# Four state-space mixers: steps of their own for the strung-out side work of the first chunk

## The chip, the cores and the metric

The kernel is one program on one core of a Trainium2 chip. The metric is the device time of the whole program in microseconds (us); for the kernel before it is 7736.49, the median of three runs (7729.43 to 7759.1).

## What is computed

The input is a batch of 64 images of 11 x 11 places and 128 channels. Four layers follow each other; each adds a mixer and then a feed-forward part to its input. The mixer is the same in all four layers, a selective state-space model that runs over 256 places (the inner channels) in two directions k, with 121 channels d (the image's places) and 16 states n:

```python
xz = x @ in_proj_w.T                         # x layer-normalised
xc, z = jnp.split(xz, 2, axis=-1)
xc = silu(conv1d(xc, conv_w) + conv_b)       # 3 taps
x_dbl = einsum('bkdl,kcd->bkcl', stack([t, t]), x_proj_w)
delta = softplus(einsum('bkrl,kdr->bkdl', dts, dt_proj_w) + dt_proj_b)
dA, dBu = exp(delta * A), delta * Bs * xs
_, h = associative_scan(_ssm_combine, (dA, dBu), axis=3)
y = einsum('bkdln,bknl->bkdl', h, Cs) + Ds * xs
y = y[:, 0] + flip(y[:, 1], axis=-1)
out = layernorm(y) * gelu(z) @ out_proj_w.T
```

The feed-forward parts (a mixture of experts, two recurrent networks, a spectral filter) are not touched by the change.

## The kernel before, in words

**Chunks, directions, steps.** A mixer (class `Conv`, method `run`) works on 8 images at a time, so there are 8 chunks. A chunk has two directions; the main loop counts them through as m = 2 x chunk + direction. In a direction the 121 channels are taken two at a time: 61 pairs, and each pair is one step of the main loop. So a chunk has 122 steps (`STEPS`) and a mixer 976. All 128 partitions hold 16 states x 8 images.

**What one step does.** TensorE (PE) spreads `delta` of a channel from the tile `R` to the 128 partitions, into one of five PSUM buffers `da` (`rows`, L686). ScalarE (ACT) takes its exponential with A as scale (`exps`, L699). This is done three steps ahead. VectorE (DVE) scans two channels at once (`scan`, L707) with `da` and `ub`, into a column of `H` or `HX`. A tile `ub` of four channels, so of two steps, is loaded by a broadcast DMA from `uD` in DRAM (`load_u`, 512 KB, ten steps ahead, six buffers), and GpSimd (POOL) multiplies it by B (`times_b`, L675, five steps ahead). A buffer of `ub` comes free when the scan of the step before the load is done, so SyncE (SP), which issues all these DMAs in program order, waits there for DVE at every second step. After every 16 steps PE multiplies the finished columns by C (`by_c`, L728) bit by bit, and ACT (first direction) or DVE (second) takes the sum out of PSUM (`keep_y`).

**What must be ready for a direction.** `dD` in DRAM holds delta as three bfloat16 parts that add up to it, `uD` holds delta x input, `bcD` holds B and C. `R`, `ub`, `Bt` and `Cp` are loaded from them (`load_r`, `load_u`, `load_bc`). The method `steps(c, k, at)` makes `dD` and `uD` for chunk c and direction k, in four parts of two images: projection on PE (`project`), a copy out of PSUM (`keep`), one softplus for all four on ACT (`soft`: a load of the activation table, the function, a load of the table for exponentials), then for each pair of images: `first`, `second` and `third` on ACT make the three parts of `d` (L329, L346, L358), `rest` and `less` on PE subtract in between, `u` on POOL (L333), and `store` issues the two DMAs to `dD` and `uD`. The tiles `d` and `u` have two buffers each, so pair 2 takes that of pair 0 and pair 3 that of pair 1.

**Side work and its places.** While chunk c is scanned, the next chunk is prepared between the scans: its input `x` is loaded (`begin`), normalised over channels (`stats` and `scales` on DVE, `scales2` and `normal` on ACT), transposed (`turn`, `turned`), convolved on PE and copied to the tile `t` (`conv`, `convd`), put through SiLU (`silu`), and then comes `steps` for both directions. The method `aside` makes B and C of the next chunk (`bc`: PE, ACT, a store) and its skip term (`skip`: a scaling on ACT into PSUM, L406, and then a combination on DVE, L409).

Each piece gets a step. `at` puts it into the plan, `lay_at` does so for a list with steps given, `lay` spreads a list evenly over a stretch and rounds down to whole steps. Within a step the main loop emits the reading-out of PSUM, the rows and first exponential of the step three ahead, the loads and B products that are due, the scan, then the plan's pieces in the order of their (fractional) steps, then the second exponential. As every engine and SP works in the order in which it is given work, a step is a place in several queues at once.

For chunks 1 to 7 the steps come from the table `AT`, with one start and one distance for each kind of piece. Chunk 0 is special: a mixer begins by making its own first direction ahead of the main loop, and the second direction (`self.steps(0, 1, ...)`) and the skip term are done within the steps of chunk 0, beside the next chunk's preparation. The steps for this stretch stand as numbers in `run`. In the list that `steps` takes, the numbers are: first projection, distance between projections, softplus, first of the splitting, distance between the pairs; relative to the pair's start, `first` comes 1, `rest` 3, `u` 4, `second` 5, `third` 7 and `store` 12.5 steps later. The normalisation's pieces come relative to their start: statistics from -3, `scales` 3, `scales2` 6, `scales3` 8, `normal` from 10, the transposes and their copies 13.5 to 19.5.

Of the kernel before, what the change touches and what calls it, by code (L numbers as in the profile page):

```python
# [70 lines left out]
def act_tables(nc, which):  # L71
# [8 lines left out]
CB = 8  # L80
# [4 lines left out]
RING = 5  # L85
UB = 6
AT = {
    "x": -12.5, "st": -3, "mv": 3, "sc2": 6, "sc3": 8, "nm": 10, "tn": 13.5, "td": 15.5, "tn2": 17.5,
    "td2": 19.5, "cv": 20, "cve": 49, "silu": 52, "p0": 53, "pa0": 3.75, "s0": 66, "b0": 66, "ba0": 7.875,
    "p1": 100, "pa1": 2.25, "s1": 109, "b1": 111, "ba1": 7.5, "u": 4, "d0": 1, "r": 3, "d1": 5, "l": 6.5,  # L90
    "d2": 7, "dst": 12.5, "bc": 54, "bca": 3, "sk": 99, "ska": 2.5, "y0": 15.5, "y1": 35, "y2": 57.5, "y3": 82,
    "k0": 27, "k1": 44.5, "k2": 66.5, "k3": 89, "ka": 2, "ks": 2.5, "km": 4.5, "k2s": 6.5, "k3s": 9, "kn": 11,
    "kg": 13, "xa": 28.5, "xb": 66, "g0": 38, "z0": 77, "g1": 81.5, "z1": 109, "ga": 5, "za": 3.5, "gt": 117.5,
    "gta": 2, "ge": 126.5, "cz": 8, "cza": 3.75, "lbc": -18, "lu": 10, "tb": 5, "ys": 8, "ysa": 1, "ysh": 8,
    "r0": -10, "r1": 2, "r2": 23, "r3": 37,
}


class Conv:
# [679 lines left out]
    def run(self):  # L779
        NC, G = self.NC, 2 * self.NC * PAIRS  # L780
        self.R, self.bc, self.ub, self.pre = {}, {}, {}, {}
        NT = 2 * NC * TILES
        first = [PAIRS * (T // TILES) + 2 * (T % TILES) for T in range(NT)]

        begin, norms, convs = self.lead(0)
        aside = self.aside(0)
        self.do([begin] + [f for _, f in norms] + convs)
        bc = [(3 * i // 3 + 1.5, f) for i, f in enumerate(aside[: 3 * CB // 2])]
        self.do([f for _, f in sorted(self.steps(0, 0) + bc, key=lambda x: x[0])])
        for x in self.da:  # L790
            self.nc.vector.memset(x[:, :, 0:1], 0.0)
        self.lay(aside[3 * CB // 2 :], 0, 20)
        self.lay_at(self.steps(0, 1, (0, 2, 9, 11, 6)))
        for c in range(NC):
            s = STEPS * c
            if c + 1 < NC:
                begin, norms, convs = self.lead(c + 1)
                aside = self.aside(c + 1)
                bc, skip = aside[: 3 * CB // 2], aside[3 * CB // 2 :]
                if c == 0:  # L800
                    self.at(2, begin)
                    self.lay_at([(18 + i, f) for i, f in norms])
                    self.lay([f for _, f in convs[:-1]], 40, 64)
                    self.at(65, convs[-1][1])
                    self.lay_at(self.steps(1, 0, (67, 2, 76, 77, 6)))
                    self.lay_at(self.steps(1, 1, (106, 2, 115, 116, 6)))
                    self.lay(bc, 78, 90)
                    self.lay(skip, 93, 104)
                else:
                    self.at(s + AT["x"], begin)  # L810
                    self.lay_at([(s + i, f) for i, f in norms + convs])
                    for k in range(2):
                        at = [s + AT[f"p{k}"], AT[f"pa{k}"], s + AT[f"s{k}"], s + AT[f"b{k}"], AT[f"ba{k}"]]
                        self.lay_at(self.steps(c + 1, k, at))
                    self.lay_at([(s + AT["bc"] + AT["bca"] * (i // 3) + i % 3, f) for i, f in enumerate(bc)])
                    self.lay_at([(s + AT["sk"] + AT["ska"] * (i // 3) + i % 3, f) for i, f in enumerate(skip)])
            self.lay_at([(s + i, f) for i, f in self.gate(c)])
            if c > 0:
                self.lay_at([(s + i, f) for i, f in self.tail(c - 1)])
        for m in range(2 * NC):  # L820
            s = PAIRS * m
            self.at(max(s + AT["lbc"], 0), lambda m=m: self.load_bc(m))
            for u in range(4):
                self.at(s + AT["cz"] + AT["cza"] * u, lambda m=m, u=u: self.own_c(m, u))
            for dq, (p0, n) in enumerate(DQ):

                before = s + AT[f"r{dq}"]
                self.at(max(before, 0), lambda m=m, dq=dq: self.load_r(m, dq))

                after = s + p0 + n  # L830
                nxt = DQ[(dq + 1) % 4][1]
                for h in range(4):
                    step, n_steps = after + h * nxt // 4, (nxt - 1) // 4 - 1 + (nxt == 16)
                    for i in range(8):
                        self.at(step + i * n_steps // 8, lambda m=m, dq=dq, slot=8 * h + i: self.by_c(m, dq, slot))
                    keep = lambda m=m, dq=dq, h=h: self.keep_y(m, dq, h)
                    step += n_steps
                    self.pre.setdefault(step, []).append(keep)
            if m % 2:
                for half in range(2):  # L840
                    for q in range(4):
                        for j in range(2):
                            self.at(
                                s + PAIRS + AT["ys"] + AT["ysh"] * half + AT["ysa"] * q,
                                lambda m=m, h=half, q=q, j=j: self.store_y(m, h, q, j),
                            )
        sides, load, ahead, finish = self.last(NC - 1)
        self.at(G + 1, sides)
        self.at(G + 12, lambda: load(0))

        early = {}
        for T in range(NT):
            for lead, f in ((AT["lu"], self.load_u), (AT["tb"], self.times_b)):
                step = first[T] - lead
                early.setdefault(max(step, -1), []).append(lambda T=T, f=f: f(T))
        self.do([f for _, f in self.plan.pop(0)])
        self.do(early.pop(-1))
        for g in range(3):
            self.rows(g)
            self.exps(g, 0)  # L860
            self.exps(g, 1)
        for g in range(G + 60):
            self.do(self.pre.pop(g, []))
            if g < G:
                if g + 3 < G:
                    self.rows(g + 3)
                    self.exps(g + 3, 0)
                self.do(early.pop(g, []))
                self.scan(g)
            self.do([f for _, f in sorted(self.plan.pop(g, []), key=lambda x: x[0])])  # L870
            if g + 3 < G:
                self.exps(g + 3, 1)
        assert not self.plan and not early and not self.pre
        ahead()
        load(1)
        X = self.cx.X
        for c in range(NC - 1):
            self.nc.sync.dma_start(X[:, CB * c : CB * c + CB, :], self.dst(CB * c, CB))
        finish()
        self.nc.sync.dma_start(X[:, CB * NC - CB :, :], self.dst(CB * NC - CB, CB))  # L880
# [614 lines left out]
```

## Time and profile before

| What | us |
|---|---|
| median of the three runs | 7736.49 |
| the profiled execution's own time | 7752.68 |
| its span, first to last instruction | 7750.9 |
| of this, before the first mixer's first scan | 69.5 |
| mixer 1, first to last scan | 1475.3 |
| feed-forward part 1 and the next mixer's beginning | 349.1 |
| mixer 2 | 1469.9 |
| feed-forward part 2 and beginning | 295.5 |
| mixer 3 | 1474.5 |
| feed-forward part 3 and beginning | 303.0 |
| mixer 4 | 1481.6 |
| feed-forward part 4 | 832.5 |

The rows between the first and the last are times between scans in the trace. PE is busy 78% of the span, DVE 73%, ACT 70% and POOL 68%; over the mixers alone (second mixer) PE is busy 1151.8 us, DVE 1294.1, ACT 1234.6 and POOL 1304.6 of 1469.9, and the 16 DMA engines 93%. Chunk by chunk, from one chunk's first scan to the next one's (the last to its last scan's end), the second mixer takes 197.7, 185.6, 183.5, 183.2, 182.7, 183.3, 180.9 and 173.0 us.

How to read this: the page counts an engine as busy while it executes, and names for its idle time what ended it. In a kernel in which all engines hand work round in a ring, the share of busy time says little; what counts is, step by step, which engine or transfer the scan waited for.

### The profile page before, as it was taken

Reading aid. Unit: us, or ns where it says so; the run is one execution under the profiler, and the core shown is the slowest. Engines: PE = TensorE matmul, PEld = TensorE weight load, DVE = VectorE, ACT = ScalarE, POOL = GpSimd, SP = SyncE. Lnnn points to the kernel's source line nnn. Section 1 sums busy time; section 2 is a strip of 40 time slices with the busy share of each in tenths; the row PEclk is TensorE's granted clock in tenths of the full one; section 3 lists DMA queues with packets and bytes.
Section 4 is the critical chain, followed back from the end, with each engine's and each line's share of the span. In section 5 each row is a group of like instructions: output and inputs, shape, how many; then the busy total and the mean of one; then the engine's idle time right before and its main releaser. Section 6 shows DMA issues by size and latency. Waiting matters only on the chain. (4 is left out here: it accounts for less than half of the span.)

```text
span 7750.9 us, 208787 instructions
## 1 busy us (share of the span) xinstructions
PE 6041.0 (78%) x84334; PEld 3448.5 (44%) x84334; DVE 5659.8 (73%) x7849; ACT 5449.4 (70%) x12343; POOL 5293.3 (68%) x2659
## 2 busy tenths in 40 slices
PE   6788778776788877766788888767678887758999
PEld 3444444465344444444344444434344444434445
DVE  5888888844788888962788888871788888872201
ACT  7888888733888888853788888862788888852200
POOL 6798999812888888931888888940888898960000
PEclk8888898777898989875889989875788888879999
DMA  7899999856899999942899999951899999971111
GB/s 181 227 247 243 245 246 243 215 167 170 221 241 249 246 240 244 247 110 75 220 241 244 246 248 243 243 140 37 217 236 243 243 245 241 245 184 46 35 39 36
DMA packets 905471, 1536.54 MB, mean 198 GB/s; under 512 B 136840, under 2 KB 617442, under 8 KB 904503
## 3 DMA queue, kind: packets, MB, share of 16 engines
q1 hardware_dynamic: 903223, 1521.09, 76.3%
q8 instruction: 662, 10.85, 0.6%
q14 instruction: 306, 2.51, 0.1%
q10 hardware_dynamic: 1280, 2.10, 0.1%
HBM read 1265.98 MB, written 256.97 MB: 196 GB/s over the span
## 5 line engine op out<-in xcount | busy, mean ns | idle before, releaser
L675 POOL TENSOR_TENSOR ub<-ub,Bt 128x1024 f32<-128x1024 f32 (+1 forms) x1984 | 4557.2, 2323 | 589.7 <-DMA ub<-uD 447.1
L699 ACT ACTIVATE da<-da,A 128x255 f32<-128x255 f32 x7744 | 3291.7, 451 | 696.1 <-PE da L686 612.0
L707 DVE TENSOR_TENSOR_SCAN H<-da,ub 128x512 f32<-128x512 f32 x2048 | 2391.8, 1208 | 354.4 <-POOL ub L675 183.9
L707 DVE TENSOR_TENSOR_SCAN HX<-da,ub 128x512 f32<-128x512 f32 (+1 forms) x1856 | 2130.4, 1190 | 318.5 <-POOL ub L675 160.1
L686 PE MATMUL da<-R,pick 120*128 120x255 bf16 x7744 | 1658.9, 305 | 546.0 <-DVE H L707 277.3
L686 PEld LDWEIGHTS <-pick 120*128 120x128 bf16 x7744 | 662.9, 103 | 1494.6 <-issue 1054.9
L728 PE MATMUL yb<-H,Cz 128*16 128x64 f32 x32768 | 782.2, 236 | 187.7 <-ACT yst L745 107.7
L728 PE MATMUL yb<-HX,Cz 128*16 128x64 f32 x32768 | 813.4, 237 | 122.6 <-DVE HX L707 62.7
L728 PEld LDWEIGHTS yb<-HX,Cz 128*16 128x16 f32 x32768 | 531.3, 105 | 641.9 <-issue 338.1
L728 PEld LDWEIGHTS yb<-H,Cz 128*16 128x16 f32 x32768 | 540.9, 103 | 584.0 <-issue 313.3
L263 PE MATMUL pc<-w_conv,xnT 128*121 128x256 f32 x1344 | 458.7, 433 | 27.4 <-ACT d L358 18.6
L184 POOL MEMSET t<- 128x2048 f32 x4 | 7.2, 1805 | 599.6 <-PE px L1221 211.8
L313 PE MATMUL pd<-t,w_dt 122*128 122x512 f32 x480 | 317.6, 749 | 101.7 <-ACT t L274 55.1
L745 ACT COPY yst<-yb 128x512 f32<-128x512 f32 (+2 forms) x640 | 334.9, 551 | 83.9 <-DMA yD<-yst 70.2
L743 DVE TENSOR_TENSOR yst<-yst,yb 128x512 f32<-128x512 f32 (+2 forms) x640 | 337.1, 543 | 73.7 <-PE yb L728 73.2
L340 PE MATMUL pr<-sp,ident 128*128 128x512 f32 x480 | 302.7, 717 | 80.0 <-ACT sp L301 75.0
L333 POOL TENSOR_TENSOR u<-sp,t 128x512 f32<-128x512 f32 x240 | 307.6, 1282 | 33.9 <-DMA uD<-u 32.8
L1294 DVE COPY U<-pu 128x488 f32<-128x488 f32 x128 | 85.4, 667 | 282.5 <-PE pu L1327 282.5
L1296 ACT COPY U<-pu 128x488 f32<-128x488 f32 x128 | 72.9, 570 | 308.7 <-PE pu L1327 308.7
L652 POOL TENSOR_TENSOR Cz<-Cp,own 128x512 f32<-128x512 f32 x256 | 275.5, 1076 | 0.0
L329 ACT CAST d<-sp 128x512 bf16<-128x512 f32 x240 | 148.6, 619 | 172.1 <-DMA dD<-d 171.9
L263 PEld LDWEIGHTS pc<-w_conv,xnT 128*121 128x121 f32 x1344 | 211.7, 194 | 94.9 <-ACT d L358 25.0
(237 smaller groups left out, 7243.8 us busy)
## 6 DMA issues: line engine op xcount, KB each, us to landing
ub<-uD SPq DMA_DIRECT2D x1920, 512.0 KB
dD<-d SPq DMA_DIRECT2D x256, 384.0 KB
R<-dD SPq DMA_DIRECT2D x192, 420.0 KB
uD<-u SPq DMA_DIRECT2D x256, 256.0 KB
yD<-yst SPq DMA_DIRECT2D x512, 60.5 KB
y<-yD SPq DMA_DIRECT2D x112, 242.0 KB
bcD<-bc SPq DMA_DIRECT2D x128, 128.0 KB
w1g<-in_L_ffn_weight_dram SPq DMA_DIRECT2D x16, 1024.0 KB
```

Of the source, the lines that this page charges most:

```text
L263: nc.tensor.matmul(pc, lhs, rhs, start=(j == 0), stop=(j == taps - 1))
L313: nc.tensor.matmul(s["p"], self.w_dt[:, k, :], tb[: D + 1], start=True, stop=True)
L333: nc.gpsimd.tensor_mul(s["u"], s["sp"], tb)
L340: nc.tensor.matmul(s["pr"], self.cx.ident, s["sp"], start=True, stop=False, skip_group_check=True)
L652: self.nc.gpsimd.tensor_mul(self.Cz[u], C.unsqueeze(2).to_broadcast([128, 64, CB]), self.own.unsqueeze(1).to_broadcast([128, 64, CB]),)
L675: self.nc.gpsimd.tensor_mul(x, x, self.bc[m, "Bt"].unsqueeze(1).to_broadcast([128, n, L]))
L686: self.nc.tensor.matmul(self.da[g % RING][:, j, 1:], self.pick[:n, d % 5].rearrange("p n b -> p (n b)"), self.R[m, d // 35][:n, d % 35 // ...
L699: self.nc.scalar.activation(x, x, AF.Exp, scale=self.A[:, m % 2, d : d + 1])
L707: self.nc.vector.tensor_tensor_scan(self.H[dq % 2][:, :n, p - DQ[dq][0]], self.da[g % RING].rearrange("p j l -> p (j l)")[:, :n], x.rearra ...
L728: self.nc.tensor.matmul(self.yb[32 * q : 32 * q + 16, slot % 8, :, :, :w], self.Cz[slot // 8][:, place % 64 : place % 64 + 2, :].rearrange ...
L743: nc.vector.tensor_add(dst, dst, src)
L745: nc.scalar.copy(dst, src)
```

## The change

The change lets the pieces of chunk 0 (its own second direction and skip term, and the preparation of chunk 1) take their steps from a table `AT0`, with a start and a distance for each kind, as `AT` has them for later chunks. The work itself, its engines and its buffers stay. `AT` is written in other lines with the same numbers; `strung` is a small function that lays three pieces a step apart and the next three by a distance of its own, as the code for later chunks did before.

```diff
+AT0 = {
+    "x": 1, "n": 10.5, "cv": 39.5, "cve": 63.5, "silu": 64, "p": 0, "pa": 2, "s": 10, "b": 10, "ba": 7, "p0": 67.5,
+    "pa0": 2.75, "s0": 78, "b0": 78, "ba0": 6.25, "p1": 104.5, "pa1": 1.875, "s1": 112.5, "b1": 113.5, "ba1": 6.625,
+    "bc": 79, "bca": 3.375, "sk": 94, "ska": 3.25, "k": 0, "ka": 3,
+}
...
-        self.lay(aside[3 * CB // 2 :], 0, 20)
-        self.lay_at(self.steps(0, 1, (0, 2, 9, 11, 6)))
+        F = AT0
+
+        def strung(fs, at, apart):
+            self.lay_at([(at + apart * (i // 3) + i % 3, f) for i, f in enumerate(fs)])
+
+        strung(aside[3 * CB // 2 :], F["k"], F["ka"])
+        self.lay_at(self.steps(0, 1, [F[x] for x in ("p", "pa", "s", "b", "ba")]))
...
-                    self.at(2, begin)
-                    self.lay_at([(18 + i, f) for i, f in norms])
-                    self.lay([f for _, f in convs[:-1]], 40, 64)
-                    self.at(65, convs[-1][1])
-                    self.lay_at(self.steps(1, 0, (67, 2, 76, 77, 6)))
-                    self.lay_at(self.steps(1, 1, (106, 2, 115, 116, 6)))
-                    self.lay(bc, 78, 90)
-                    self.lay(skip, 93, 104)
+                    self.at(F["x"], begin)
+                    self.lay_at([(F["n"] + i, f) for i, f in norms])
+                    apart = (F["cve"] - F["cv"]) / (len(convs) - 1)
+                    self.lay_at([(F["cv"] + i * apart, f) for i, (_, f) in enumerate(convs[:-1])])
+                    self.at(F["silu"], convs[-1][1])
+                    for k in range(2):
+                        self.lay_at(self.steps(1, k, [F[x + str(k)] for x in ("p", "pa", "s", "b", "ba")]))
+                    strung(bc, F["bc"], F["bca"])
+                    strung(skip, F["sk"], F["ska"])
```

Step by step, in chunk 0:

| Piece | before | after |
|---|---|---|
| own skip (DVE half) | 1, 6, 11, 16 | 1, 4, 7, 10 |
| own softplus | 9 | 10 |
| own splitting, start and distance | 11, 6 | 10, 7 |
| chunk 1: load of x | 2 | 1 |
| chunk 1: normalisation's start | 18 | 10.5 |
| chunk 1: convolutions | 40 to 63 | 39.5 to 62.8 |
| chunk 1: SiLU | 65 | 64 |
| chunk 1, first direction: projections | 67, then every 2 | 67.5, then every 2.75 |
| softplus; splitting | 76; 77, every 6 | 78; 78, every 6.25 |
| second direction: projections | 106, then every 2 | 104.5, then every 1.875 |
| softplus; splitting | 115; 116, every 6 | 112.5; 113.5, every 6.625 |
| chunk 1: B and C, stores at | 80, 83, 86, 89 | 81, 84.375, 87.75, 91.125 |
| chunk 1: skip (DVE half) | 93, 96, 99, 102 | 95, 98.25, 101.5, 104.75 |

## The prediction

> **What bounds the kernel now.** I read the table of slices first, then the scans (L707) one by one, then the waits and the timeline where their pace breaks. Each mixer runs 976 scans, 122 per chunk of 8 images; I call the stretch from one scan's start to the next a step and count from the mixer's first scan.
>
> ```profile
> DVE  5888888844788888962788888871788888872201
> ACT  7888888733888888853788888862788888852200
> POOL 6798999812888888931888888940888898960000
> DMA  7899999856899999942899999951899999971111
> ```
>
> The four plateaus are the mixers. Inside one, chunk 0 takes longest: 196.2, 197.7, 196.9 and 197.7 us from its first scan to chunk 1's, where chunk 4 takes 183.0, 182.7, 183.5 and 183.6. So the place of this change is four stretches of 197 us, 10% of the run. Stage by stage, in the second mixer (columns: the window and its length; busy us of PE, weight loads, DVE, ACT, POOL with counts; granted clock, DMA share, GB/s):
>
> ```profile
> 1893.90:1926.00 32.10, 19.33 (x114) 8.86 (x114) 26.84 (x33) 25.52 (x53) 28.86 (x15) 0.61 0.97 225
> 1926.00:1952.40 26.40, 18.54 (x301) 9.35 (x299) 18.89 (x26) 18.75 (x47) 25.35 (x14) 0.77 0.82 218
> 1952.40:1992.40 40.00, 37.23 (x640) 22.06 (x639) 35.16 (x32) 33.18 (x77) 34.21 (x16) 0.96 0.97 252
> 1992.40:2021.30 28.90, 19.21 (x298) 8.29 (x299) 16.93 (x15) 25.23 (x51) 26.41 (x15) 0.82 0.64 165
> 2038.50:2066.10 27.60, 16.52 (x251) 8.21 (x251) 20.45 (x22) 17.94 (x42) 19.93 (x10) 0.72 0.79 208
> 2066.10:2091.70 25.60, 20.09 (x342) 9.48 (x341) 21.94 (x29) 19.82 (x41) 16.69 (x9) 0.90 0.96 233
> 2091.70:2277.20 185.50, 148.16 (x2533) 83.98 (x2535) 163.79 (x208) 161.24 (x365) 165.97 (x84) 0.90 0.94 242
> ```
>
> The rows are steps 0 to 20, 20 to 35, 35 to 66, 66 to 80, 92 to 106, 106 to 122, and all of chunk 1. The last row shows the limit of a good stretch: DMA at 0.94. In chunk 0 DMA is free in steps 20 to 35, 66 to 80 and 92 to 106 (0.82, 0.64, 0.79) and full around them. Time can be won only where DMA is free: by my sum of its packets 6.4 us of idle lie in steps 15 to 35, 13.1 in 65 to 85, 6.1 in 90 to 105. What stands there are in-order queues. The second mixer's chunk 0, ACT's and DVE's waits:
>
> ```profile
> ACT da L699 <- PE da L686: 21.6, 22, 2.2
> ACT d L329 <- DMA dD<-d: 15.6, 3, 5.6
> ...
> DVE H L707 <- ACT da L699: 7.3, 5, 4.2
> DVE skip L409 <- ACT ps L406: 6.7, 3, 4.8
> DVE HX L707 <- POOL u L333: 4.4, 1, 4.4
> ...
> DVE r L202 <- ACT r L198: 4.0, 1, 4.0
> ```
>
> Two kinds are to be seen. ACT has to copy image pair 2 into the buffer of pair 0 (two buffers of d) and waits three times, 5.6 us at most, for pair 0's store. And DVE has strung work (skip, r) ahead of its scans that waits for ACT:
>
> ```profile
> 1909.50 1.91 ACT L301 ACTIVATE sp<-sp 128x2048 f32<-128x2048 f32 x1
> 1911.43 1.28 ACT L73 ACT_TABLE_LOAD   x1
> ...
> 1914.17 0.75 DVE L409 SCALAR_TENSOR_TENSOR skip<-t,Ds,ps 121x512 f32<-121x512 f32 x1 [4.77 <-ACT ps L406]
> ```
>
> The softplus with its two table loads (1.28 + 1.91 + 1.28 us) holds ACT for 4.5 us; the skip behind it holds the scans.
>
> **Part by part.** No instruction is added or removed; the sums are of waits. Rows are the second mixer's.
>
> (a) *Own skip and the next chunk's statistics, ahead of the softplus.* Skips go from steps 1, 6, 11, 16 to 1, 4, 7, 10, the eight bn_stats from 15-18 to 7-10, the softplus from 9 to 10. DVE then does two more skips (0.73 us each) and eight bn_stats (0.28 each), 3.7 us, before the block, so its wait of 4.77 falls to about 1.1: 3.7 won. Their data: the load of x moves from step 2 to 1 and so ahead of the ub load that waits for scan 1; it is issued at about 1889.2 and not 1896.94. In the queue it then lands behind the sixth ub (1902.41), by 3 us as now behind the seventh (1905.06, x at 1908.11): 1905.5, where the first bn_stats comes up at 1905.2. The ub load pushed back (1905 to about 1907) feeds scan 12 and has 4 us to spare.
>
> (b) *The first d wait.* Before, pair 2's copy stands at step 24 and pair 0's store at 23.5, behind a load of R; now 25 and 22.5, ahead of it. One step (1.1 us) and R's turn (it landed 1.7 us after the ub ahead of it) take ACT's 5.58 to 2.8. The r chain that held DVE 3.97 us is done at step 18.5, before this wait; the scans then lose about 1.1: 2.9 won.
>
> (c) *The eight normalisations on ACT* (0.49 each) go from steps 28-31, where three d copies (0.6) fall, to 20-23, where one does. The scans' waits there (0.50, 0.32, 1.45, 0.86) go from 3.1 to about 1.5: 1.6 won.
>
> (a) to (c) add up to 8.2, but what is late next is DMA (idle 6.4, of which some stays) and POOL: from 1912.1, when the eighth ub has landed, it works almost without a break, and its last product for scan 36 is ready at 1946.7, when scan 36 starts at 1953.5: 6.7 at most. I take **4.2** (3.0 to 5.4); the first mixer has only 3.7 us of DMA idle in steps 10 to 35 (others 6.8), there 2.3. The convolutions behind (39.5 to 63.5 for 40 to 64) do not move: 0.
>
> (d) *The next chunk's projections* go from every 2 steps to every 2.75. In steps 73-77 scans wait 1.98, 0.67 and 0.56 us, while PE stands 2.25 and 1.04 us at a projection whose one PSUM buffer ACT has yet to empty. Of 3.2 I take **1.2** (0 to 3.2); ACT, 25.2 busy of 28.9, allows 3.7.
>
> (e) *SiLU at 64 for 65, softplus at 78 for 76*: their blocks (scan waits 4.16 and 4.36) only move: **0** (-0.5 to 0.8).
>
> (f) *Second and third d wait, and the skips, steps 90 to 105.* Pair 2's copy is at step 91 for 90, pair 3's at 97 for 96, the stores stay between the same ub loads, the first without a bc store ahead of it (0.6). Scans 93 and 99 lost 2.83 and 2.40 and lose 1.7 and 1.1 less. POOL's u of pairs 2 and 3 (94.5 and 100.75 for 93 and 99) now comes behind that step's ub product, not ahead of it, when it waits for its store (1.4 and 3.9 us). The skips stand a step behind ACT's half and no longer in the same one: of 1.38 + 0.54, 1.5 goes. Together **4.3** (2 to 6, DMA's idle).
>
> (g) *The second softplus at 112 for 115* follows its copies by one step, not two; its wait was 1.17 and could become the 4.36 of the first: **-0.5** (-3.2 to 0.5).
>
> (h) *The last stores.* The own one goes from 41.5 to 43.5, read from 51 on: it lands 7 us after issue, 9 steps are left: 0. The next chunk's goes from 107.5 to 109.25, and the first ub load of chunk 1 waits for it on SP with all loads behind. That load is issued 6.45 us after the load the store now follows, the store needs 6.5 to 7.9 us: **-0.3** (-4.4, at the longest landing, 10.87, to 0).
>
> (i) *Chunk 1's copies* (pair 3 two steps behind pair 1's store, not one): **0.5** (0 to 1.2, DMA's idle in steps 122 to 150).
>
> Weighed against a page: the Trainium skill, page "DMA: Bandwidth & Descriptors", section "Anatomy of one DMA", fits one DMA alone at 2.0 us plus bytes at 436 GB/s, an estimate of 2.9 us for a d store. Here these stores land after 5.3 to 8.9 us. By the page the waits left in (f) would go too, 2.4 us more a mixer, and the sum would be 7691; I go by the rows.
>
> **The sum.** 4.2 + 1.2 + 0 + 4.3 - 0.5 - 0.3 + 0.5 = 9.4 us in three mixers, 7.5 in the first: 35.7. The profiled execution took 7752.68 us (span 7750.9, 1.8 around it) and would take 7717.0; it lies 16.2 above the median of the runs, 7736.49. These stalls return in every mixer alike, so I take them off the median: **7701**, 0.46% faster. About 0.5% (38.7 us, so 7697.8 and 7775.2) is what a measurement of this kernel can tell from no change; the forecast lies just inside.
>
> **Rivals.**
> *Chunk 0 reaches chunk 4's pace* (chance 0.25): the terms add up beyond my caps. 788.5 us now, 732.8 at that pace: 55.7 won, 7681. For it: chunk 4 has SiLU and softplus too, and more DMA; against it: the two blocks of (e) keep 8.5 us a mixer.
> *DMA gives it back* (0.18): steps 35 to 66 run at DMA 0.97, and what (a) to (c) win is waited for there. Only (d) to (i) stay, 5.2 x 4 = 21: 7716.
> *The hand-over loses* (0.06, slower): if waits of (f) only move on, chunk 1's first load hangs on a store that is issued two steps (2.9 us) later, or by 4.4 us if it lands as late as the longest. It decides once the store needs more than 6.45 us and the gains ahead are under this price: up to 4.4 x 4 = 18 lost, 7754.
> *DVE and POOL get in each other's way* (0.02): 3.7 us of DVE work move into steps 0 to 10, where POOL has no idle time. If POOL stood still meanwhile, 14.8 of the sum would go: 7716. The ub products beside a skip took 2.38 us on average, beside scans alone 2.37, so nothing bears it out. The Trainium skill, page "Advanced Engine Details and Errata", section "VectorE Performance Modes", has such a rule: VectorE's second port is shared with GpSimd, and instructions that use both block each other.
>
> The forecast itself has 0.47 (7685 to 7716). Range: 7668 to 7738, from the first rival with 13 us of scatter (the three runs lie up to 23 us from their median) to no change. Under 7697.8 lie two fifths of the forecast's chance and the first rival's: faster 0.46, same 0.49, slower 0.05.
>
> **What would show it.** (a) no skip waits over 1 us before step 20, r none at all; (b) ACT's d wait before step 30 under 3 us; (c) steps 20 to 35 at 23 us or less; (d) steps 66 to 80 at 28; (f) steps 92 to 106 at 24; (h) chunk 1's first scan with no wait for ub longer than now. Wrong would make it: bn_stats waiting for x, PE waiting at step 104 for pair 3's last copy (103.75), or chunk 1 growing by what chunk 0 shrinks.

## The result, and the profile after

The kernel after takes 7690.02 us, the median of four runs (7687.08 to 7695.77); the kernel before has 7741.39 over its four runs (7729.43 to 7759.1). The ratio is 0.9929, with an interval of 0.9918 to 0.9941: 0.7% faster, 51 us (46 from the median of three that the forecast started from). The forecast was 7701 and 36 us, its range 7668 to 7738.

Line numbers are four higher than before: L699 is L703, L707 is L711, L329 is L333. The slices of the profile after:

```profile
DVE  6889888844888888962888888871888988872201
ACT  7888888734888888843888888852888888852200
POOL 6899888812899999921988889940888989860000
DMA  7999999856999999932999999951899999961111
```

They look as before; the change is too small for slices. Chunk by chunk it shows: chunk 0 now takes 180.2, 183.3, 182.6 and 187.4 us in the four mixers, 733.4 in all and 55.0 less than before. That is the pace of the chunks behind it. Another 12 us fell in the steps of chunk 1 up to 150. These 67 us are more than the 51 of the medians: the profiled execution before took 7752.68 us, 11 over its median, and between the mixers the one after took 5 us longer. So the stages below, added up, give some 30% more than the medians do. Stage by stage, the second mixer after (the same steps and columns as the rows of before, chunk 1 last):

```profile
1872.60:1902.80 30.20, 20.11 (x112) 8.38 (x112) 28.31 (x41) 24.31 (x51) 26.91 (x14) 0.50 1.00 230
1902.80:1924.40 21.60, 16.35 (x307) 8.56 (x306) 17.59 (x16) 21.10 (x52) 21.60 (x12) 0.97 1.00 269
1924.40:1965.00 40.60, 36.38 (x636) 22.33 (x635) 35.77 (x32) 32.70 (x75) 39.19 (x19) 1.00 1.03 254
1965.00:1988.00 23.00, 18.30 (x298) 8.74 (x298) 16.79 (x17) 21.07 (x47) 21.83 (x12) 0.78 0.72 191
2008.10:2031.20 23.10, 17.05 (x278) 8.34 (x279) 20.26 (x23) 17.97 (x42) 20.04 (x10) 0.85 0.85 249
2031.20:2055.90 24.70, 16.67 (x314) 8.79 (x312) 21.65 (x29) 18.98 (x38) 16.87 (x9) 0.93 0.92 242
2055.90:2239.70 183.80, 148.67 (x2537) 83.65 (x2537) 163.89 (x209) 162.22 (x366) 165.23 (x83) 0.90 0.93 244
```

Steps 20 to 35 fall from 26.4 to 21.6 us, with POOL busy all the time and DMA at 1.00. Steps 66 to 80 fall from 28.9 to 23.0, but part of that is only moved: the softplus that held them stands two steps later and its block now falls into steps 80 to 92, which go from 17.1 to 20.1. Steps 92 to 106 fall from 27.6 to 23.1. The waits of ACT and DVE in chunk 0 of the second mixer after:

```profile
ACT da L703 <- PE da L690: 18.3, 22, 2.0
ACT d L333 <- DMA dD<-d: 5.9, 3, 4.4
...
DVE HX L711 <- POOL ub L679: 4.5, 4, 1.8
DVE yst L747 <- PE yb L732: 3.9, 3, 2.0
...
DVE H L711 <- POOL ub L679: 2.4, 2, 1.2
...
DVE skip L413 <- ACT ps L410: 0.5, 2, 0.3
DVE st L229 <- DMA x<-mid: 0.4, 1, 0.4
```

ACT's wait for the buffer of d is down from 15.6 to 5.9 us, the skip's from 6.7 to 0.5, the wait of r is gone. New are waits of the scans for POOL's products (6.9 together) and a short one of the statistics for x.

Mean us of the four mixers, from each run's profile, by steps (the columns e1 to e12 are the experiments below; e9 is the kernel after once more):

| steps | before | after | e1 | e2 | e3 | e4 | e5 | e6 | e7 | e8 | e9 | e10 | e11 | e12 |
|---|---|---|---|---|---|---|---|---|---|---|---|---|---|---|
| 0-20 | 31.5 | 30.4 | 30.5 | 31.6 | 30.9 | 31.5 | 30.7 | 30.4 | 30.6 | 30.5 | 30.9 | 30.4 | 32.2 | 30.6 |
| 20-35 | 25.6 | 21.8 | 21.8 | 24.9 | 21.3 | 21.3 | 21.7 | 21.9 | 22.0 | 21.8 | 22.0 | 22.0 | 20.4 | 24.1 |
| 35-66 | 40.4 | 39.7 | 39.1 | 40.6 | 41.4 | 40.0 | 39.4 | 40.4 | 39.4 | 40.4 | 39.4 | 39.5 | 39.9 | 40.2 |
| 66-92 | 46.2 | 43.6 | 47.0 | 43.5 | 43.7 | 47.1 | 43.4 | 46.0 | 43.6 | 43.5 | 43.6 | 43.4 | 43.5 | 43.5 |
| 92-106 | 27.7 | 23.0 | 27.3 | 23.0 | 22.7 | 20.1 | 21.0 | 22.9 | 24.8 | 22.6 | 23.3 | 21.1 | 22.6 | 23.1 |
| 106-122 | 25.7 | 24.8 | 26.2 | 24.2 | 24.6 | 25.4 | 23.4 | 23.7 | 23.3 | 26.6 | 24.3 | 23.4 | 24.0 | 24.6 |
| 122-150 | 45.9 | 43.0 | 44.8 | 43.2 | 43.7 | 41.8 | 40.8 | 44.0 | 42.6 | 45.1 | 43.7 | 40.3 | 43.7 | 45.0 |

A column is one execution. The two of the kernel after differ by up to 0.7 us in a row, and steps 0 to 66 take 91.9 to 92.8 us in the five kernels whose places there are the same (after, e6 to e9). The profiled executions of e3, e4 and e11 lay 11, 17 and 29 us under their runs' medians, that of e12 lay 19 over.

### The profile page after: what moved, and what is told of

Read it like the earlier page. It is cut to its first block, busy times and chain, and to the rows that moved or that the text cites. A ratio compares the mean times of both kernels' runs of the same rounds, so it can differ in the third digit from the quotient of the medians.

```text
span 7688.9 us, 208815 instructions
## 1 busy us (share of the span) xinstructions
PE 6015.5 (78%) x84334; PEld 3447.4 (45%) x84334; DVE 5664.0 (74%) x7849; ACT 5464.8 (71%) x12343; POOL 5292.7 (69%) x2659
## 4 chain that ended last, share of the span: by engine, by line
PE 29%; ACT 19%; DMA 17%; DVE 14%; issue 11%; POOL 8%; SPq 1%; DVEq 0%; POOLq 0%; ACTq 0%
ACT da L703 10%; DMA ub<-uD 8%; POOL ub L679 6%; DVE H L711 5%; DVE HX L711 5%; PE yb L732 4%; DMA dD<-d 4%; PE da L690 3%; PE acc L1340 3%; PE pu L1337 3%; PE out L1380 3%; PE pc L267 3%; PE pst L1224 2%; DVE yst L747 1%; ACT yst L749 1%
## 5 line engine op out<-in xcount | busy, mean ns | idle before, releaser
L703 ACT ACTIVATE da<-da,A 128x255 f32<-128x255 f32 x7744 | 3306.4, 453 | 675.7 <-PE da L690 590.5
L711 DVE TENSOR_TENSOR_SCAN H<-da,ub 128x512 f32<-128x512 f32 x2048 | 2396.9, 1210 | 344.8 <-POOL ub L679 162.2
L711 DVE TENSOR_TENSOR_SCAN HX<-da,ub 128x512 f32<-128x512 f32 (+1 forms) x1856 | 2132.2, 1192 | 277.5 <-POOL ub L679 160.9
L267 PE MATMUL pc<-w_conv,xnT 128*121 128x256 f32 x1344 | 452.9, 430 | 24.9 <-ACT d L362 18.4
L333 ACT CAST d<-sp 128x512 bf16<-128x512 f32 x240 | 149.1, 621 | 118.8 <-DMA dD<-d 118.6
```

The costliest lines, as they stand in the source:

```text
L267: nc.tensor.matmul(pc, lhs, rhs, start=(j == 0), stop=(j == taps - 1))
L703: self.nc.scalar.activation(x, x, AF.Exp, scale=self.A[:, m % 2, d : d + 1])
L711: self.nc.vector.tensor_tensor_scan(self.H[dq % 2][:, :n, p - DQ[dq][0]], self.da[g % RING].rearrange("p j l -> p (j l)")[:, :n], x.rearra ...
```

## The experiments

The theory: in-order queues made chunk 0 wait, the most for a store that frees a buffer of d too late, and each piece's new place takes a wait away. Rivals: DMA gives the front's gain back; or the d wait only covers other waits that stand behind it. Each group ran beside the kernel before on one chip, on which that took 7759.0 (e1 to e4), 7763.8 (e5 to e8) and 7766.5 (the last four). So ratios to the kernel before are compared, with intervals; microseconds in the expectations stand for the first chip.

**e1, the front alone.** The kernel after with all that follows step 35 as before:

```diff
-                    apart = (F["cve"] - F["cv"]) / (len(convs) - 1)
...
-                    strung(skip, F["sk"], F["ska"])
+                    self.lay([f for _, f in convs[:-1]], 40, 64)
+                    self.at(65, convs[-1][1])
+                    self.lay_at(self.steps(1, 0, (67, 2, 76, 77, 6)))
+                    self.lay_at(self.steps(1, 1, (106, 2, 115, 116, 6)))
+                    self.lay(bc, 78, 90)
+                    self.lay(skip, 93, 104)
```

> Only the first 35 steps take their new places (own skip, own softplus and splitting, load of x, normalisation); convolutions and all that follows keep the old ones. If the terms add (a to c each take a wait away), steps 0 to 35 shrink as in the kernel after, by 2.4 us in the first mixer and about 5.6 in the others, 19 us in all: 7722. The prediction's own capped terms say 15: 7726. If DMA gives it back in steps 35 to 66, nothing is left at the end of chunk 0: 7741.

Measured: 0.9964 (0.9947 to 0.9981). Steps 0 to 35 take 52.3 us for 57.1, and steps 35 to 66 give nothing back (39.1 for 40.4). At the end of chunk 0, 5.3 us a mixer are left. DMA does not give the front back.

**e2, the rest alone.** The other half:

```diff
-    "x": 1, "n": 10.5, "cv": 39.5,
+    "x": 2, "n": 18, "cv": 39.5,
...
-        strung(aside[3 * CB // 2 :], F["k"], F["ka"])
-        self.lay_at(self.steps(0, 1, [F[x] for x in ("p", "pa", "s", "b", "ba")]))
+        self.lay(aside[3 * CB // 2 :], 0, 20)
+        self.lay_at(self.steps(0, 1, (0, 2, 9, 11, 6)))
```

> The other half: the first 35 steps keep their old places, convolutions and all that follows take the new ones. If the terms add: 51 less 19, so 32 us faster, 7709, with steps 66 to 92 at 43.5 us for 46 and steps 92 to 106 at 23 for 27.6. If the front is given back by DMA and the whole gain comes from here: 7690.

Measured: 0.9956 (0.9940 to 0.9973), with steps 66 to 92 and 92 to 106 as in the kernel after. The halves, 0.36% and 0.44%, add up to the whole, 0.71%, within their intervals.

**e3, no early skip and normalisation.** The kernel after with these two at their old places:

```diff
-    "x": 1, "n": 10.5, "cv": 39.5,
+    "x": 2, "n": 18, "cv": 39.5,
...
-        strung(aside[3 * CB // 2 :], F["k"], F["ka"])
+        self.lay(aside[3 * CB // 2 :], 0, 20)
```

> The kernel after, with the own skip and the next chunk's load of x and normalisation at their old steps; the own splitting keeps its distance of 7. If (a), (c) and the r chain are what the front gains, 14 us are lost: 7704, and the skip's wait of over 3 us stands in step 11 again. If the front's gain is the distance between pairs (the d wait) alone: 7691.

Measured: 0.9931 (0.9915 to 0.9947), the ratio of the kernel after. Steps 20 to 35 take 21.3, and steps 0 to 35 take 52.2 us, as in the kernel after; steps 0 to 66 take 93.6 us for 91.9. What the prediction held to be most of the front's gain (a, c and the r chain) is worth 1.7 us a mixer, twice the scatter of like kernels, and shows behind step 35 alone.

**e12, the old own splitting.** The counterpart of e3:

```diff
-    "s": 10, "b": 10, "ba": 7,
+    "s": 9, "b": 11, "ba": 6,
```

> The kernel after, with the own softplus at 9 and the own splitting at 11, 6 apart, as before; own skip, load of x and normalisation keep their new places. If the distance between store and copy is what the front gained (as the run without the early skip says): steps 20 to 35 at 25 us for 21.8 and 3 to 4 us a mixer lost, 0.995. If early skip and normalisation alone would do as well: 0.993.

Measured: 0.9949 (0.9932 to 0.9967). Steps 20 to 35 go back to 24.1, steps 0 to 66 to 94.9. ACT's wait for d in steps 20 to 35 of the second mixer, in e12 and in e3:

```profile
ACT d L333 <- DMA dD<-d: 4.3, 2, 3.4
```

```profile
ACT d L333 <- DMA dD<-d: 1.9, 1, 1.9
```

In steps 0 to 66 the own splitting's new places (softplus, start and distance, which this edit moves together) carry the larger part: 97.5 us before, 93.6 with them alone (e3), 94.9 with early skip and normalisation alone (e12), 91.9 with both. The ratios of e3 and e12 point the same way, but their intervals overlap. That it is the time between store and copy, and not the softplus's place, is shown by e4.

**e4, the kernel before with earlier stores.** One number, for the three strung-out stages alone:

```diff
-                out += [(b0 + ba * i + AT[n], f) for n, f in ...]
+                out += [(b0 + ba * i + (9.5 if n == "dst" and c < 2 else AT[n]), f) for n, f in ...]
```

> The kernel before, with one number changed: the stores of the three strung-out stages stand 9.5 steps behind their pair's start and not 12.5. Nothing else moves. If ACT's wait for the buffer of d is what costs in steps 20 to 30 and 90 to 100 and in chunk 1's first 20 steps, these waits go and 6 to 8 us a mixer are won: 7713. If the wait only covers others behind it (r, skip, u): 7735 or no change.

Measured: 0.9929 (0.9910 to 0.9948). This single number wins as much as the whole change. ACT's and DVE's waits in chunk 0 of the second mixer, with this run's skip and softplus where they were before:

```profile
ACT d L329 <- DMA dD<-d: 1.7, 2, 0.9
```

```profile
DVE skip L409 <- ACT ps L406: 4.8, 1, 4.8
DVE HX L707 <- POOL u L333: 4.4, 1, 4.4
```

The d wait falls from 15.6 to 1.7 us. With the stores alone moved, steps 0 to 66 take 92.8 us and steps 106 to 150 take 67.2, nearly as in the kernel after (91.9 and 67.8). The wait of r and the skip's waits at steps 93 and 99 go with it, though neither was moved; the skip behind the own softplus waits 4.8 as ever. Steps 92 to 106 take 20.1 us, 2.9 less than in the kernel after:

```profile
2025.40:2045.40 20.00, 12.85 (x249) 6.59 (x249) 20.00 (x22) 16.39 (x39) 18.79 (x9) 0.90 0.96 284
```

DVE is busy 20.00 of 20.00 us there: no scan waits at all. So the d wait does not merely cover other waits; others hung on it.

**e5, the kernel after with earlier stores.** The same edit in the kernel after.

> The kernel after, with the stores of the strung-out stages 9.5 steps behind their pair's start and not 12.5. What is left of the d wait there (scan waits of 1.4 to 3.6 us in step 94, 0.6 to 2 in step 130, 1.4 to 2.8 in step 137) should go: up to 5 us a mixer, 7670. If DMA is by now what ends these stretches: 7690, and the waits are for ub instead.

Measured: 0.9907 (0.9886 to 0.9928). Steps 92 to 106 and 106 to 150 lose another 2.0 and 3.6 us. The ratio's interval overlaps that of the kernel after, so this gain is read from the stages.

**e6, projections every 2 steps again.**

```diff
-    "p0": 67.5, "pa0": 2.75,
+    "p0": 67, "pa0": 2,
```

> The kernel after, with the next chunk's first projections at 67 and every 2 steps again, the softplus still at 78. By term (d) of the prediction 1.2 us a mixer are lost: 7695. By what steps 66 to 92 gained in all (2.6): up to 7700. If only the softplus's place counts there: 7690.

Measured: 0.9946 (0.9925 to 0.9966). Steps 66 to 92 are back at 46.0, from 43.6: nearly their whole gain is the projections' places, 2.4 us a mixer.

**e7, pairs of the first direction 6 apart.**

```diff
-    "ba0": 6.25,
+    "ba0": 6,
```

> The kernel after, with the pairs of the next chunk's first direction 6 steps apart and not 6.25, from the same start (78). Pair 2's copy then stands at step 91 as now, pair 3's at 97, but u of pair 2 at 94 and of pair 3 at 100, the stores at 90.5, 96.5, 102.5 and 108.5. If the gain of (f) comes from the step that the copies have gained: 7690. If it comes from the place of u behind that step's product: the order stays too, 7690; if from the distance itself, up to 2 us a mixer: 7698.

Measured: 0.9928 (0.9910 to 0.9945), not to be told from the kernel after. Its stage shows it nonetheless: steps 92 to 106 take 24.8 for 23.0, while steps 106 to 122 are 1.5 shorter.

**e8, the old second direction.**

```diff
-    "p1": 104.5, "pa1": 1.875, "s1": 112.5, "b1": 113.5, "ba1": 6.625,
+    "p1": 106, "pa1": 2, "s1": 115, "b1": 116, "ba1": 6,
```

> The kernel after, with the next chunk's second direction (projections, softplus, splitting) at its old steps 106, 115, 116 and 6 apart. By terms (g), (h) and (i) of the prediction these places are worth nothing in chunk 0 and 0.5 us in chunk 1: 7691. By what steps 106 to 150 gained in all (about 3.8 a mixer): 7705.

Measured: 0.9944 (0.9925 to 0.9964). Steps 106 to 150 take 71.7 us for 67.8: these places are worth 3.9 us a mixer (3.1 over the first three mixers; e8's fourth is long, 75.6), not nothing. In the second mixer the waits of chunk 1 at steps 132 and 138 (2.5 and 3.6 us) are back.

**e9, the kernel after on this chip:** unchanged.

> The kernel after once more, unchanged, so that the runs beside it can be set against it on one chip: 0.993 of the kernel before.

Measured: 0.9931 (0.9913 to 0.9949).

**e10, early stores in every chunk.**

```diff
-    "d2": 7, "dst": 12.5,
+    "d2": 7, "dst": 9.5,
```

> The kernel after, with every chunk's stores 9.5 steps behind their pair's start, not those of the strung-out stages alone. In chunks 2 to 7 of the kernel after ACT still waits some 20 us a mixer for d (about ten waits). If those reach the scans, up to 20 us a mixer more than the 0.9907 of the run with early stores in chunk 0 alone: 0.981 to 0.985. If DMA or POOL covers them, as the share of DMA there (0.92 to 0.98) suggests: 0.990.

Measured: 0.9880 (0.9865 to 0.9895), the fastest of all, and clear of the kernel after beside it. ACT's waits in the second mixer behind step 150, in the kernel after:

```profile
ACT da L703 <- PE da L690: 115.4, 187, 2.8
ACT d L333 <- DMA dD<-d: 17.7, 10, 3.1
```

and in e10:

```profile
ACT da L703 <- PE da L690: 140.6, 205, 2.9
```

The d wait is gone from the list, 17.7 us. But ACT waits 25 us longer for PE's rows, and the steps from 150 on differ by only 3.2 us a mixer from e9 (1232.8 for 1236.0). These 3.2 are no sign of a gain: the kernels that have the same places from step 150 on take 1229.3 to 1240.2 there. So there ACT's wait for d was covered, as far as these profiles can tell. Of the 10.5 us a mixer that e10 wins on e9, 7.3 lie before step 150, where e5's gain lies too.

**e11, the own u on DVE.**

```diff
-                nc.gpsimd.tensor_mul(s["u"], s["sp"], tb)
+                (nc.vector if c == 0 and k == 1 else nc.gpsimd).tensor_mul(s["u"], s["sp"], tb)
```

> The kernel after, with the own second direction's four products u (1.3 us each on POOL) made by DVE. POOL is busy all of steps 20 to 35 and the scans wait for its products at steps 22, 26, 28, 34 and 42, 5.2 us in all. If POOL is what the removed waits of the front have turned into, these go and steps 20 to 50 shrink by 3 to 5 us a mixer: 0.991. If DMA (share 1.00 there) is, POOL waits for ub instead and nothing changes: 0.993.

Measured: 0.9942 (0.9925 to 0.9958), not faster. The scans' waits in steps 0 to 66 of the second mixer:

```profile
DVE HX L711 <- ACT da L703: 2.8, 4, 0.9
DVE H L711 <- ACT da L703: 1.4, 3, 0.6
```

Behind the first scan none waits for POOL any more, but DVE has four products more to do, and steps 0 to 66 stay at 92.5 us (91.9 after). Steps 20 to 35 fall to 20.4, but steps 0 to 20 grow from 30.4 to 32.2. The products take 1.31 us on average over the four mixers, from 0.66 to 2.87, and the long ones stand beside a product of POOL that had just begun. Two in the second mixer:

```profile
1907.09 5.12 POOL L679 TENSOR_TENSOR ub<-ub,Bt 128x1024 f32<-128x1024 f32 x2
1907.27 2.72 DVE L337 TENSOR_TENSOR u<-sp,t 128x512 f32<-128x512 f32 x1
...
1917.80 0.66 DVE L337 TENSOR_TENSOR u<-sp,t 128x512 f32<-128x512 f32 x1
```

Of the 16 products, 15 begin while POOL works on a product, and each of these ends 0.55 to 0.56 us after the one then running. The nine ub products that begin during one take 2.67 to 2.85 us; the other 1911 have a median of 2.38, and none takes more than 2.6. So DVE and POOL held each other up here, and e11 does not tell which of POOL, DVE and DMA alone would be the bound.

A third buffer for d and u, which might have taken the wait away with no store moved, was not tried.

## Why the prediction was right, and where its sizes were off

The direction, the range and the main mechanism (ACT's waits for the buffer of d, and strung work ahead of the scans) were right; the sum was 36 us where 51 came, and by its chances no telling change (0.49) stood a little ahead of faster (0.46). The first rival, chunk 0 at the pace of chunk 4, is what happened: it said 55.7 us less in chunk 0, and 55.0 it was by the profiles (7681 by its sum, 7690 measured).

**(a) to (c), the front.** Forecast 4.2 us (2.3 in the first mixer), capped from 8.2. Measured in steps 0 to 35: 2.4 in the first mixer, 6.6, 5.5 and 4.8 in the others. That the front has a cap is so, and it lies a little over the 5.4 that was taken for it: steps 20 to 35 take 21.3 to 22.0 us in ten of the eleven kernels whose own d wait is shortened (e11, with POOL relieved, reaches 20.4), and DMA stands at a share of 0.99 to 1.00 and 269 to 271 GB/s there in four of them (after, e4, e5, e10; means of four mixers). What the terms beneath the cap were worth was misjudged. (a) did shrink the skip's wait, from 4.8 to a scan wait of 1.1, but the moved work showed in steps 0 to 10, which grew from 13.1 to 15.1 us; (a), (c) and r together are worth 1.7 (e3, behind step 35), the d wait most of the rest (e4). The bn_stats waited for x for 0.4 to 1.4 us; 0.3 was forecast.

**(d) was too small:** 1.2 forecast, 2.4 measured (e6). Of the scan waits of 1.98, 0.67 and 0.56 in the second mixer 0.85 and 0.19 are left.

**(e) was right:** the blocks only moved. The second costs 2.5 us at step 81 and 2.0 at step 83, not 4.4, 1.0 and 0.8.

**(f) had the right size and a wrong working.** 4.3 forecast, 4.7 measured. But e4 wins 7.6 in these steps with skip and u where they were, so the 1.5 for the skip's place and the better order of u were no terms of their own: their waits came and went with ACT's.

**(g), (h) and (i) failed as a sum:** -0.3 together, +3.9 measured (e8). By the stages most of the missing 15 us are theirs. The softplus's wait grew by 0.6 as forecast. (h)'s wait for the last store came: in all four mixers after, chunk 1's first ub load is issued 0.1 us after that store has landed (before, in the first mixer alone). SyncE's wait for it in the second mixer after:

```profile
SPq L667 <- DMA uD<-u: 4.7, 1, 4.7
```

PE's weight loads wait at step 118 or 119 for the R that is loaded behind it, 1.5 to 4.0 us; before, 2.2 to 3.5. In e10, where that load is issued 2.8 to 2.9 us after the landing, steps 106 to 122 take 23.4 us for 24.8; how much of this is (h)'s is not shown.

The step that fell is (i): "0.5 (0 to 1.2, DMA's idle in steps 122 to 150)". The scan waits there, 2.2 to 2.8 at step 132 and 3.3 to 5.6 at step 138, were d waits like the others and fell to 0.6 to 2.0 and 1.4 to 2.8; with the stores alone moved (e4) they are 0.5. The cap was taken from DMA's busy share, by the premise that "Time can be won only where DMA is free", and that share was no floor. Steps 122 to 150 of the second mixer before, after and in e10:

```profile
2091.70:2137.30 45.60, 33.53 (x525) 18.10 (x524) 36.33 (x49) 37.04 (x83) 41.28 (x23) 0.81 0.98 248
```

```profile
2055.90:2099.40 43.50, 32.23 (x552) 17.92 (x552) 36.22 (x48) 38.90 (x88) 38.20 (x20) 0.92 0.93 237
```

```profile
2056.60:2097.10 40.50, 31.40 (x551) 17.53 (x549) 36.11 (x48) 37.43 (x85) 36.97 (x20) 0.92 0.97 247
```

At a share of 0.98 five microseconds could still be won.

**How long a store takes.** The stores of chunk 0 land 5.4 to 7.8 us after issue in the second mixer after, and of the waits in (f) 1.4 to 3.6 us are left at step 94. The Trainium skill, page "DMA: Bandwidth & Descriptors", section "Anatomy of one DMA", gives its fit for transfers that GpSimd issues. By its 2.9 us for a d store, an estimate, the waits would have gone (7691); the measurement decides against it. The stores here are issued by SyncE.

**VectorE beside GpSimd.** The work that was moved shows no such hindrance: the ub products beside the moved skips and statistics (steps 9 to 12) take 2.36 to 2.37 us, as those beside scans alone, and in the whole run after the skips take 0.72 to 0.75 us and the bn_stats 0.27 to 0.30. But the rival's mechanism is there for other work: it is what e11 shows for DVE's product of two SBUF tiles (0.66 to 2.87 us). The Trainium skill, page "Advanced Engine Details and Errata", section "VectorE Performance Modes", says that two-port instructions of VectorE and instructions of GpSimd block each other. Its table gives this instruction no two-port mode, so the measurement goes further than the page.

**By the signs that were named:** no skip waits over 1 us before step 20 and r waits nowhere; ACT does not wait for d before step 30 (under 3 us was named); steps 20 to 35 are at 21.8 (23 or less was named), steps 66 to 80 at 23 (28; their softplus has left them), steps 92 to 106 at 23.0 (24); chunk 1's first scan waits for no ub. Of the signs against it two came faintly: bn_stats waits for x (0.4 to 1.4 us), and PE for pair 3's last copy (0.8 us at most). Chunk 1 did not grow (184.8 us in the mean, 186.1 before).

## What to carry to other kernels

Where a buffer goes round through a store, look at the distance in time between the store's issue and the next writing of that buffer, against the store's measured landing (here 5 to 9 us): if it is shorter, the writing engine stops, and with it all that is queued behind it, and other pieces' waits show up in the list that are none of their own. Moving the store, one number, won here as much as a whole table of new places, and both together won more than either (0.9880, with the store moved in every chunk). A wait that stands out is worth an experiment that takes it alone away before the pieces around it are moved.

## What was not expected of the hardware

A DMA share near 1 does not tell how fast bytes can go. By the mean of four mixers, steps 35 to 66 of the kernel after move 255 GB/s at a share of 1.00, its steps 20 to 35 move 271 at 0.99, and steps 92 to 106 of e4 move 284 at 1.00; steps 122 to 150 go from 45.9 us at 0.95 (before) to 40.3 at 0.94 (e10), with 10.9 and 10.1 MB moved. So these stretches had room that the share does not show; which transfers make the difference, no run separates.

VectorE's multiplication of two SBUF tiles and GpSimd's do not run freely beside each other: in e11 the one on VectorE took 0.66 us where GpSimd's was nearly done and up to 2.87 us where it had just begun, and GpSimd's then took 2.67 to 2.85 us for 2.38. Scans and skips, which read one operand from PSUM, kept their times in the run after (scans 1.21 us with a GpSimd instruction beside them and without, skips 0.72 to 0.75).
